# Layer 0's channel-by-row tile: VectorE block transposes of a second load in place of TensorE transposes

## The chip, the cores and the metric

The kernel runs on one core of one Trainium2 chip. The metric is the device time of one execution in microseconds; the time of a kernel is the median of several executions. The core has five engines that run side by side, each through its own queue of instructions in order: TensorE (PE, with its weight loads shown apart as PEld), VectorE (DVE), ScalarE (ACT), GpSimd (POOL) and SyncE (SP), which issues most of the transfers. Transfers of one issuing queue run on 16 shared DMA engines. An instruction waits for semaphores that others set.

## The reference

The input `x` has 128 rows (`s`) of 256 tokens (`i`) of 256 channels. Two layers of the form `x = x + layer(group_norm(x))` follow each other:

```python
# layer 0: 8 heads of 32 channels, bias from z, gate
m_norm = layer_norm(m)                       # m = group_norm(x), 32 groups of 8 channels
q, k, v = m_norm @ Wq.T, m_norm @ Wk.T, m_norm @ Wv.T
b = layer_norm(z) @ Wb.T                     # z: 256 x 256 x 128, one bias per head
p = softmax(q @ k.T / sqrt(32) + b)          # over the 256 tokens of one row s
o = (p @ v) * sigmoid(m @ Wg.T + bg)
x = x + o @ Wo.T + bo
# layer 1: 4 heads of 64 channels, only keys within 16 tokens
x = x + attention(group_norm(x))
```

All numbers are float32. The group norm of layer 0 needs one mean and one scale per channel over the whole of `x`; the layer norm after it needs one root per token (`lrs`).

## The kernel before

The program has a fast path and a general one; a verdict computed at the end of the fast path decides whether the general one runs as well. Only the fast path runs here, and it has four stages.

First, until about 240 us, the stage over `z`: 16 jobs load 2 MB of `z` each, take statistics on DVE (`z_front`), turn the data on PE and project it to the bias (`z_back`), and leave the exponential of the bias in `eb`. Between the jobs `x` is read once for its group moments. Small steps are hung into this stage by a table, `plan`, whose key says after which job and at which quarter of its DVE work a step is issued: among them `norm`, which takes the rows `M0` and `R0` (mean and scale of each channel, the same on all partitions), and the turn of pair 0. Weights are prepared here too.

Second, the loop of layer 0, one iteration for each of the 64 pairs of rows. Its order is written out by hand under a manual schedule: what an engine does follows the order of the calls. Four pairs are under way in an iteration: `old` and `was` are being finished, `now` is in its attention, `nxt` is being prepared, and `nn` is being centred. A pair passes through these steps:

- its construction loads `xt`, 512 rows (tokens) on partitions in four tiles of 128, by one 512 KB DMA (L1225); token 2p+b of a row lies on partition p;
- `centre` and `scale` (L1233, L1236) form `xg` = (x - M) R on POOL;
- `moments` takes mean and variance of each token on DVE, `root` the root on POOL, `send` writes the 512 roots to DRAM (`rs_d`, L1259), and `fetch` reads them back, the same on every partition, as `rs_r` (L1264);
- `turn` makes `xgT`, channels on partitions: eight 128x128 transposes on PE into PSUM tile `ps_x` (L1274), copied out by ACT (L1278);
- `normal` multiplies `xgT` with `rs_r` on POOL (L1283), which gives `xnT`; the weights have been centred, so that subtracting the token's mean isn't needed;
- `project` (L1296) makes `qT` and `kT` from `xnT` and the gate `gT` from `xgT`, `values` (L1311) makes `v` from `xnT`;
- `scores(r, c)` (L1330) and the exponential on ACT (L1337), `add_bias`: product with `eb` on DVE (L1346) and sum over the two token halves on POOL (`eboth`, L1351); `apply` (L1362, L1370) makes the weighted values and the attention sums `su`;
- `gate`, then `invert`: reciprocal of the sums on DVE (L1383), written to DRAM (`rsum`, L1384) and read back by four DMAs as `rvb` (L1391);
- `normalize` on POOL (L1407), `out_row` on PE (L1417), `keep_row` on DVE (L1424), and a 2 MB store of `x1` every fourth pair (L1430).

The scores' PSUM tiles and `ps_x` share two buffers; `xg`, `xgT`, `xnT` and `rs_r` have two buffers each, `xt` five. SP issues in this order in an iteration: roots written, sums written, sums fetched (four), roots fetched, store of `x1` if any, next `xt`.

Third, a short passage with the group moments of layer 1. Fourth, the loop of layer 1. It gets its channel-major tile without PE: `xs` is loaded in runs of 32 channels by four DMAs a pair, one for each band of 32 partitions (L1720), and VectorE's transpose (L1730), which turns 32x32 blocks, finishes it; ACT then subtracts the mean (L1735).

Of the kernel before, what the change touches and what calls it, by code (L numbers as in the profile page):

```python
# [9 lines left out]
F32 = mybir.dt.float32  # L10
AF = mybir.ActivationFunctionType
ALU = mybir.AluOpType
# [4 lines left out]
P = 128  # L17
# [4 lines left out]
def bcast(ap, axis, n):  # L22

    ap = ap.unsqueeze(axis)
    shape = list(ap.shape)
    shape[axis] = n
    return ap.broadcast_to(shape)
# [746 lines left out]
def fast_kernel(  # L774
# [25 lines left out]
    nc = tc.nc  # L800
    S, I, C = x.shape
    CZ = z.shape[2]
    H = wbT.shape[1]
    D0 = C // H
# [3 lines left out]
    NB = I // P  # L808
    KC = C // P
    NP = S // 2  # L810
    N2 = 2 * I
# [4 lines left out]
    const = ctx.enter_context(tc.tile_pool(name="const", bufs=1))  # L816
    dram = ctx.enter_context(tc.tile_pool(name="dram", bufs=1, space=DRAM))

    ident = const.tile([P, P], F32, name="ident")
# [111 lines left out]
    for a in range(KC):  # L931
        for h in range(H1):
            n = P // H1
# [5 lines left out]
    for h in range(H1):  # L939
        n = P // H1  # L940
# [57 lines left out]
    def mm(name):  # L998
        return ps_mm.tile([P, 512], F32, name=name, tag="mm")
# [199 lines left out]
    HQ = P // D0  # L1199
    NT = 2 * NB  # L1200
# [11 lines left out]
    for n in range(RC):  # L1212
# [2 lines left out]
            bcast(ident.rearrange("p (q d) -> p q d", q=HQ)[:, :, n * D0 // RC], 2, D0),  # L1215
        )

    class Pair:


# [7 lines left out]
            )  # L1228


        def centre(self):
            self.xg = la.tile([P, NT, C], F32, name="xg", tag="xg", bufs=2)
            nc.gpsimd.tensor_tensor(self.xg, self.xt, bcast(M0, 1, NT), ALU.subtract)  # L1233

        def scale(self):
# [145 lines left out]
        def invert(self):  # L1381
            rv = self.rv = lb.tile([P, I], F32, name="rv", tag="rv", bufs=2)
            nc.vector.reciprocal(rv, su)  # L1383
            nc.sync.dma_start(  # L1384
                rsum[self.p].rearrange("q r c i -> (q r c) i"), rv[0 : P : D0 // RC]
            )
            if self.p == NP - 1:
                return
            self.rvb = lb.tile([P, 2, KC, I], F32, name="rvb", tag="rvb", bufs=2)
            for q in range(HQ):  # L1390
                nc.sync.dma_start(  # L1391
                    self.rvb[q * D0 : (q + 1) * D0].rearrange("p r c i -> p (r c i)"),
                    rsum[self.p, q].rearrange("r c i -> (r c i)").unsqueeze(0).broadcast_to([D0, RC * I]),
                )
# [67 lines left out]
    def some(n):  # L1462
        for _ in range(min(n, len(later))):
            later.pop(0)()
# [10 lines left out]
    def pair(p):  # L1475
        return Pair(p) if p < NP else Nobody()
# [20 lines left out]
    def norm():  # L1497
        nonlocal M0, R0, nxt
        M0, R0 = next(steps)
        now.centre()  # L1500
        now.scale()
        nxt = pair(1)

    def weigh():
# [5 lines left out]

    plan = {
        (0, 4): begin, (1, 1): lambda: next(steps), (1, 3): lambda: next(steps), (1, 4): take, (2, 3): norm,
        (3, 4): weigh,
        (5, 3): lambda: now.send(nc.scalar),
# [13 lines left out]
    behind, nx, n = None, 0, 0  # L1528
# [39 lines left out]
    su = ps_o.tile([P, I], F32, name="ps_su")  # L1568

    with tc.manual_schedule():  # L1570
        old = was = Nobody()
        es = nn3 = None
        for p in range(NP):

            nxt.root()
            nxt.send()
            e0 = now.add_bias(0, 0, now.scores(0, 0))
            was.apply(1, es)
            was.gate(1)
            was.invert()  # L1580
            nxt.fetch()
            nn.centre()
            if p == 0:
                nxt.residual()
            now.project("qT", 1)
            now.project("kT", 1)
            some(1 if p < NP - 2 else 3)
            now.values(0)
            now.keep_values(0)

            es = e0, now.add_bias(0, 1, now.scores(0, 1))
            nn.scale()
            if p == 0:
                now.residual()
            for m in range(KC):
                now.project("gT", m)
            old.out_row(1)
            some(1 if p < NP - 2 else 3)
            old.keep_row(1)

            nn3 = pair(p + 3)
            e0 = now.add_bias(1, 0, now.scores(1, 0))
            now.apply(0, es)
            now.gate(0)
            nxt.turn()
            nxt.normal()
            was.normalize(0)
            now.values(1)
            now.keep_values(1)
            nn.moments(0)  # L1610
            if p == NP - 1:
                some(8)

            es = e0, now.add_bias(1, 1, now.scores(1, 1))
            was.normalize(1)
            nn.residual()
            nxt.project("qT", 0)
            nxt.project("kT", 0)
            nn.moments(1)
            some(3 if p < NP - 2 else 9)  # L1620
            was.out_row(0)
            was.keep_row(0)
            old, was, now, nxt, nn = was, now, nxt, nn, nn3
        was.apply(1, es)
        was.gate(1)
        was.invert()
        old.out_row(1)
        was.spread()
        old.keep_row(1)
        for r in range(2):  # L1630
            was.normalize_last(r)
        for r in range(2):
            was.out_row(r)
            was.keep_row(r)
        some(len(later))
# [29 lines left out]
    with tc.tile_pool(name="l1", bufs=2) as sb, tc.tile_pool(  # L1665
        name="l1s", bufs=4
    ) as sm, tc.tile_pool(name="ps1_mm", bufs=2, space=PSUM) as ps_mm, tc.tile_pool(
        name="ps1_s", bufs=1, space=PSUM
    ) as ps_s, tc.tile_pool(name="ps1_o", bufs=1, space=PSUM) as ps_o:

        def mm1(name):
            return ps_mm.tile([P, 512], F32, name=name, tag="mm")
# [174 lines left out]
        def pair1(p):  # L1847
            return Pair1(p) if p < NP else Nobody()
# [15 lines left out]
        with tc.manual_schedule():  # L1864
            now, nxt = pair1(0), pair1(1)
# [18 lines left out]
        with tc.manual_schedule():  # L1884
            was = Nobody()
            for p in range(NP - 1):
                nn = pair1(p + 2) if p == 0 else n3
# [27 lines left out]
                was, now, nxt = now, nxt, nn  # L1915
# [19 lines left out]
        ps = mm1("ok_ps")  # L1935
# [4 lines left out]
@with_exitstack  # L1940
def mixer_kernel(ctx, tc, *args):

    nc = tc.nc
    keep = ctx.enter_context(tc.tile_pool(name="verdict", bufs=1))
    verdict = keep.tile([1, 1], mybir.dt.int32, name="verdict")
    fast_kernel(tc, *args, verdict)
    again = nc.values_load(verdict[0:1, 0:1], min_val=0, max_val=1)
    with tc.If(again > 0):
        general_kernel(tc, *args)
# [53 lines left out]
```

## Time and profile before

| what | value |
|---|---|
| time, median of 3 (lowest to highest) | 3313.72 us (3311.55 to 3315.22) |
| the profiled execution's own time | 3316.03 us |
| span of its profile | 3314.3 us |
| mean granted clock of TensorE | 0.982 |
| PE, share of the span | 95% |
| DVE | 64% |
| POOL | 59% |
| ACT | 44% |
| share of PE in the chain that ended last | 91% |

The shares are means over stages that differ. The profile's 40 slices of 83 us each show three parts: two and a half slices in which the DMA engines are nearly full (the stage over `z` and the first reading of `x`), slices 3 to 24 for layer 0, and the rest for layer 1, with a dip of PE between the two layers. The chain of work that ended last is followed back from the last instruction, at each step to what released it, so its lines say what set the time: the projections of layer 0 (L1296) hold 21% of the span in it, the scores (L1330) 8%, and PE's transposes `ps_x` (L1274) 2%.

Of the operations that the change touches, the trace of before has these: 512 transposes on PE, 8 for each of the 64 pairs; 128 copies of `xgT` by ACT, 589 ns each; and, in layer 1, 256 block loads and 64 block transposes.

### The profile page before, as it was taken

The numbers are of one execution on the slowest core, as the hardware profiler recorded it, in microseconds if no ns is written. First come the engines' busy times: TensorE is split into PE (matmuls) and PEld (weight loads), VectorE is DVE, ScalarE is ACT, GpSimd is POOL, SyncE is SP. The second block draws the span as 40 slices with busy tenths as digits, with TensorE's granted clock in tenths as the row PEclk, the third lists the DMA queues.
The fourth block names the chain that finished last, engine by engine and source line by source line (L and its number), as shares of the span: only waits on it lengthen the run. The fifth ranks groups of instructions, "written<-read, shape, count | busy, mean of one in ns | idle before, by whom it ended". The sixth has DMA issues, their size and how long they took to land.

```text
span 3314.3 us, 80768 instructions
## 1 busy us (share of the span) xinstructions
PE 3157.9 (95%) x34656; PEld 1977.2 (60%) x34656; DVE 2121.6 (64%) x3179; ACT 1452.7 (44%) x2121; POOL 1962.8 (59%) x1375
## 2 busy tenths in 40 slices
PE   5389999999999999999999999699999999999998
PEld 3255555555555555555555555466666666666666
DVE  7955666666666666666666666466655555555566
ACT  2264444444444444444444444244444444444443
POOL 2378777777787777787887776233333333333332
PEclk8699999999999999999999999899999999999999
DMA  9951212212221222222122211533333434343431
GB/s 354 375 137 43 75 49 75 75 46 65 72 75 49 75 75 60 64 64 69 49 75 75 75 49 52 104 79 91 85 90 86 92 85 91 85 92 84 92 90 54
DMA packets 464879, 295.92 MB, mean 89 GB/s; under 512 B 312480, under 2 KB 413728, under 8 KB 463360
## 3 DMA queue, kind: packets, MB, share of 16 engines
q1 hardware_dynamic: 459440, 287.76, 31.7%
q8 instruction: 275, 4.51, 0.6%
q10 hardware_dynamic: 5072, 2.90, 0.3%
q14 instruction: 92, 0.75, 0.1%
HBM read 221.85 MB, written 68.75 MB: 88 GB/s over the span
## 4 chain that ended last, share of the span: by engine, by line
PE 91%; DVE 3%; DMA 3%; ACT 1%; POOL 1%; SPq 1%; issue 0%; ACTq 0%; POOLq 0%; DVEq 0%
PE ps_p L1296 21%; PE ps_p L1745 14%; PE ps_sc L1330 8%; PE ps_y L1833 7%; PE ps_ov L1362 7%; PE ps_v L1760 7%; PE ps_y L1417 7%; PE ps_v L1311 6%; PE ps_o L1802 3%; PE ps_su L1370 3%; PE ps_sc L1774 3%; PE ps_x L1274 2%; PE ps_su L1802 1%; DVE st L1178 1%; DVE zst L1103 1%; DMA zt<-in_z_dram 1%
## 5 line engine op out<-in xcount | busy, mean ns | idle before, releaser
L1351 POOL TENSOR_TENSOR eboth<-e 128x512 f32<-128x512 f32 x512 | 640.6, 1273 | 392.9 <-DVE e L1346 389.7
L1346 DVE TENSOR_TENSOR e<-ps_sc,eb 128x1024 f32<-128x1024 f32 x512 | 603.1, 1219 | 307.0 <-ACT ps_sc L1337 306.9
L1337 ACT ACTIVATE ps_sc<-ps_sc 128x1024 f32<-128x1024 f32 x512 | 492.8, 1006 | 509.2 <-PE ps_sc L1330 509.2
L1784 POOL TENSOR_TENSOR e<-e,bw 128x384 f32<-128x384 f32 x256 | 259.5, 1035 | 769.8 <-ACT e L1782 769.8
L1745 PE MATMUL ps_p<-xgT,w_in 128*128 128x512 f32 x1024 | 470.3, 602 | 4.5 <-issue 3.7
L1745 PEld LDWEIGHTS ps_p<-xgT,w_in 128*128 128x128 f32 x1024 | 190.1, 191 | 203.7 <-issue 174.8
L1330 PE MATMUL ps_sc<-qT,kT 32*128 32x256 f32 x4096 | 293.3, 400 | 2.1 <-ACT kT L1300 2.1
L1296 PE MATMUL ps_p<-xnT,wq 128*128 128x512 f32 x512 | 267.3, 634 | 3.5 <-POOL xnT L1283 3.1
L1833 PE MATMUL ps_y<-w_out,oT 128*128 128x256 f32 x1024 | 250.3, 388 | 2.6 <-DVE oT L1818 2.6
L1837 DVE TENSOR_TENSOR yo<-ps_y,xt 128x512 f32<-128x512 f32 x128 | 88.4, 690 | 251.9 <-PE ps_y L1833 149.7
L1362 PE MATMUL ps_ov<-e,v 128*32 128x256 f32 x4096 | 247.7, 382 | 0.0
L1417 PE MATMUL ps_y<-wo,oT 128*128 128x256 f32 x1024 | 242.1, 379 | 2.0 <-POOL oT L1407 1.2
L1417 PEld LDWEIGHTS ps_y<-wo,oT 128*128 128x128 f32 x1024 | 194.3, 190 | 82.5 <-issue 59.3
L1311 PE MATMUL ps_v<-wv,xnT 128*128 128x256 f32 x1024 | 242.2, 379 | 0.0
L1330 PEld LDWEIGHTS ps_sc<-qT,kT 32*128 32x128 f32 x4096 | 184.9, 184 | 94.4 <-issue 83.6
L1296 PE MATMUL ps_p<-xnT,wk 128*128 128x512 f32 x512 | 240.8, 592 | 0.0
L1296 PE MATMUL ps_p<-xgT,wg 128*128 128x512 f32 x512 | 236.8, 605 | 0.0
L1760 PE MATMUL ps_v<-w_in,xgT 128*128 128x256 f32 x1024 | 231.8, 379 | 0.0
L1815 DVE RECIPROCAL rv<-odd 128x256 f32<-128x256 f32 x128 | 224.4, 1753 | 4.4
L1760 PEld LDWEIGHTS ps_v<-w_in,xgT 128*128 128x128 f32 x1024 | 194.4, 190 | 53.5 <-issue 30.1
L1317 DVE TENSOR_TENSOR v<-ps_v,vb_r 128x512 f32<-128x512 f32 x128 | 88.6, 692 | 206.8 <-PE ps_v L1311 206.8
L1311 PEld LDWEIGHTS ps_v<-wv,xnT 128*128 128x128 f32 x1024 | 189.6, 190 | 50.8 <-issue 31.0
(169 smaller groups left out, 4989.9 us busy)
## 6 DMA issues: line engine op xcount, KB each, us to landing
xa<-in_x_dram SPq DMA_DIRECT2D x8, 4096.0 KB
xt<-in_x_dram SPq DMA_DIRECT2D x64, 512.0 KB
x<-xo SPq DMA_DIRECT2D x16, 2048.0 KB
xs<-x SPq DMA_DIRECT2D x256, 128.0 KB
xt<-x SPq DMA_DIRECT2D x64, 512.0 KB
rvb<-rsum SPq DMA_DIRECT2D x252, 128.0 KB
out_dram<-yo SPq DMA_DIRECT2D x63, 512.0 KB
zt<-in_z_dram SPq DMA_DIRECT2D x15, 2048.0 KB
```

The costliest lines, as they stand in the source:

```text
L1296: nc.tensor.matmul(ps, w[:, k, m * P : (m + 1) * P], getattr(self, src)[:, k, :], start=(k == 0), stop=(k == KC - 1),)
L1311: nc.tensor.matmul(self.ps_v[:, b * C : (b + 1) * C], self.xnT[:, k, t * P : (t + 1) * P], wv[:, k, :], start=(k == 0), stop=(k == KC - 1),)
L1330: nc.tensor.matmul(self.pss[q // 2][:, q % 2, b, :], self.kT[rs, c, r * I + b * P : r * I + (b + 1) * P], self.qT[rs, c, r * I : (r + 1) * I],
L1337: nc.scalar.activation(self.pss[a], self.pss[a], AF.Exp)
L1346: nc.vector.tensor_tensor(e, pss[a], eb[:, h : h + 2], ALU.mult)
L1351: nc.gpsimd.tensor_tensor(t, es[a][:, :, 0, :], es[a][:, :, 1, :], ALU.add)
L1362: nc.tensor.matmul(ov[q * D0 : (q + 1) * D0, c, :], self.v[:, r, b, h * D0 : (h + 1) * D0], es[q // 2][:, q % 2, b, :], start=(b == 0), st ...
L1417: nc.tensor.matmul(self.ps_y[:, b * C : (b + 1) * C], self.oT[r][:, k, b * P : (b + 1) * P], wo[:, k, :], start=(k == 0), stop=(k == KC - 1),)
L1745: nc.tensor.matmul(ps, w_in[:, k, n * C + m * P : n * C + (m + 1) * P], self.xgT[:, k, :], start=(k == 0), stop=(k == KC - 1),)
L1760: nc.tensor.matmul(ps[:, b * C : (b + 1) * C], self.xgT[:, k, t * P : (t + 1) * P], w_in[:, k, 2 * C : 3 * C], start=(k == 0), stop=(k == ...
L1784: nc.gpsimd.tensor_tensor(e[:, q], e[:, q], bcast(bw.rearrange("p b w -> p (b w)"), 1, KC), ALU.mult)
L1833: nc.tensor.matmul(ps[:, b * C : (b + 1) * C], self.oT[r][:, k, b * P : (b + 1) * P], w_out[:, k, :], start=(k == 0), stop=(k == KC - 1),)
```

## The change

Layer 0 gets its channel-major tile in the way that layer 1 does. Each pair from the second on is loaded a second time, as `xs`, in runs of 32 channels (`blocks`: four DMAs of 128 KB); two VectorE transposes make `xgT` from it (`turn_blocks`), and ACT applies the group norm, R x - R M, with its per-partition scale and bias (`scale_blocks`). For that, R and -R M are needed as columns: `norm` makes them in `col` by four products on PE and two small DVE instructions. `turn` is no longer called in the loop; pair 0 is still turned on PE in the stage over `z`. `xg` remains, for the statistics of the tokens, with one buffer instead of two. `xs` has one buffer: the block load of `nn` is issued after the transposes of `nxt`. The loop's order changes in three more places: `normal` comes before `scores(1, 0)` instead of after `gate(0)`; `invert` ends with the write of the sums, and their four fetches form `fetch_sums`, called after `fetch`.

```diff
+    col = const.tile([P, 2, KC], F32, name="col")
...
+        def blocks(self):
+            self.xs = la.tile([P, NB, KC, 2 * HQ, D0], F32, name="xs", tag="xs", bufs=1)
+            by_block = x[2 * self.p : 2 * self.p + 2].rearrange(
+                "s (i b n) (k j a) -> j b (n k) (s i) a", i=HQ, n=NB, k=KC, a=D0
+            )
+            for j in range(HQ):
+                nc.sync.dma_start(self.xs[j * D0 : (j + 1) * D0].rearrange("b n k i a -> b (n k) i a"), by_block[j])
+
+        def turn_blocks(self):
+            self.xgT = la.tile([P, KC, N2], F32, name="xgT", tag="xgT", bufs=2)
+            for n in range(NB):
+                nc.vector.transpose(
+                    self.xgT.rearrange("p k (s n i b) -> p n k s i b", s=2, n=NB, i=HQ)[:, n],
+                    self.xs[:, n].rearrange("p k (s i) a -> p k s i a", s=2),
+                )
+
+        def scale_blocks(self):
+            for k in range(KC):
+                nc.scalar.activation(
+                    self.xgT[:, k, :], self.xgT[:, k, :], AF.Identity,
+                    bias=col[:, 1, k : k + 1], scale=col[:, 0, k : k + 1],
+                )
...
-            self.xg = la.tile([P, NT, C], F32, name="xg", tag="xg", bufs=2)
+            self.xg = la.tile([P, NT, C], F32, name="xg", tag="xg", bufs=1)
...
-            if self.p == NP - 1:
-                return
+
+        def fetch_sums(self):
             self.rvb = lb.tile([P, 2, KC, I], F32, name="rvb", tag="rvb", bufs=2)
...
         M0, R0 = next(steps)
+        ps = mm("ps_col")
+        for n, row in enumerate((R0, M0)):
+            for k in range(KC):
+                nc.tensor.matmul(
+                    ps[:, n * KC + k : n * KC + k + 1], row[:, k * P : (k + 1) * P], ident[:, 0:1],
+                    start=True, stop=True,
+                )
+        nc.vector.tensor_copy(col[:, 0], ps[:, 0:KC])
+        nc.vector.scalar_tensor_tensor(col[:, 1], ps[:, KC : 2 * KC], -1.0, col[:, 0], ALU.mult, ALU.mult)
...
     with tc.manual_schedule():
+        nxt.blocks()
...
             nxt.fetch()
+            was.fetch_sums()
             nn.centre()
...
             now.keep_values(0)
+            nxt.turn_blocks()
+            nn.blocks()
...
                 now.project("gT", m)
+            nxt.scale_blocks()
...
+            nxt.normal()
             e0 = now.add_bias(1, 0, now.scores(1, 0))
             now.apply(0, es)
             now.gate(0)
-            nxt.turn()
-            nxt.normal()
             was.normalize(0)
```

## The prediction

> **What bounds the kernel now.** I read the windows view first, for the stretch in which layer 0 runs its loop over pairs of rows. Its columns are busy time and instruction counts of PE, PEld, DVE, ACT and POOL, then the granted clock, the DMA share and GB/s.
>
> ```profile
> 330.00:2038.00 1708.00, 1707.15 (x13259) 1000.24 (x13258) 1136.27 (x1718) 764.99 (x950) 1350.32 (x947) 1.00 0.23 65
> ```
>
> PE has work in 1707.15 of 1708.00 us at full clock; POOL has 79%, DVE 67%, ACT 45%, the DMA engines 23%. A busy PE is not always an advancing PE, so I next read the timeline of one pair (start, duration, engine, line, operation), and took from it the distances between the starts of PE's groups.
>
> ```profile
> 1004.30 1.05 PE L1370 MATMUL ps_su<-eboth,pick 128*32 128x256 f32 x16
> 1005.28 1.09 PE L1274 MATMUL ps_x<-ident,xg 128*128 128x128 f32 x8
> 1006.21 1.89 PE L1311 MATMUL ps_v<-wv,xnT 128*128 128x256 f32 x8
> 1008.03 1.15 PE L1330 MATMUL ps_sc<-qT,kT 32*128 32x256 f32 x16
> 1009.11 2.17 PE L1296 MATMUL ps_p<-xnT,wq 128*128 128x512 f32 x4
> 1010.16 0.30 PEld L1296 LDWEIGHTS ps_p<-xnT,wq 128*128 128x128 f32 x2 [0.75 <-POOL xnT L1283]
> 1011.12 1.88 PE L1296 MATMUL ps_p<-xnT,wk 128*128 128x512 f32 x4
> ...
> 1018.46 1.98 PE L1296 MATMUL ps_p<-xnT,wq 128*128 128x512 f32 x4
> 1020.28 1.88 PE L1296 MATMUL ps_p<-xnT,wk 128*128 128x512 f32 x4
> ```
>
> Two things are to be seen. The eight transposes hold PE from 1005.28 to 1006.21, 0.93 us. The wait ahead of them is nothing: from the sums' start to theirs is 0.98 us, and where `wq` follows the sums (1017.48 to 1018.46, same view) it is also 0.98. And the first `wq` group takes 2.01 us (1009.11 to 1011.12) where the other takes 1.82: it waits 0.19 us for the second half of `xnT`. The same groups return every 28.77 us, all through the loop, so PE's order of work sets this stage, and only what shortens that order counts.
>
> **What the Trainium skill says.** "VectorE: DVE Perf Modes", section "The three transpose paths": VectorE turns 32x32 blocks only, into SBUF. That is why the load must place 32-channel runs on four bands of partitions; layer 1 of this trace does the same (L1720, L1730). Same page, section on the TRN2 errata: an instruction with SBUF sources pays a fixed latency, so that half a tile costs more than half; its formula for another operation, (N+151)/0.96, gives as an estimate 0.69 us for 512 elements. No row here shows a 512-element block transpose. "DMA: Bandwidth & Descriptors", section "Why small descriptors are slow": a fixed overhead per packet. Layer 1's 128-byte packets show its size here: in one pair (2600 to 2618.6 us) 4096 of them took 55.0 us together, 13.4 ns each. Same page, section "Anatomy of one DMA — SWDGE (gpsimd) path": completion of a write to HBM waits for its receipt. The trace agrees: `rs_d`, issued at 1018.68, is complete at 1026.86 by its semaphore, 8.2 us for 2 KB.
>
> **The change, part by part.** The slots it uses in the same pair:
>
> ```profile
> 1023.93 0.69 DVE L1317 TENSOR_TENSOR v<-ps_v,vb_r 128x512 f32<-128x512 f32 x1 [2.15 <-PE ps_v L1311]
> ...
> 1026.11 2.36 DVE L1346 TENSOR_TENSOR e<-ps_sc,eb 128x1024 f32<-128x1024 f32 x2 [1.49 <-ACT ps_sc L1337]
> ...
> 1028.63 0.69 ACT L1300 ACTIVATE gT<-ps_p,bg_c 128x512 f32<-128x512 f32 x1 [1.03 <-PE ps_p L1296]
> 1029.68 0.37 SPq L1264 DMA_DIRECT2D rs_r<-rs_d  x1
> 1029.93 2.36 POOL L1236 TENSOR_TENSOR xg<-xg,R_l 128x1024 f32<-128x1024 f32 x1
> 1030.25 1.15 PE L1330 MATMUL ps_sc<-qT,kT 32*128 32x256 f32 x16
> ```
>
> *TensorE transposes out.* 63 loop iterations turn a next pair (pair 0 keeps its turn): 63 x 0.93 = 58.6 us less.
>
> *`normal` moved up,* past `scores(1,0)` and the bias product, on POOL past the two `eboth` sums of (1,0). It now starts when `scale` ends, 1032.3, and ends at 1034.8; PE wants `xnT` at about 1036.9. The 0.19 us wait goes: 62 x 0.2 = 12.4 us. The first pair has a larger one: `xnT` there ends at 263.0 and PE starts `wq` at 261.86 instead of about 259.1; with `normal` 2.5 us earlier, 2.7 us come back. The `eboth` pair is 2.5 us later; PE reads it in the next iteration's `apply(1)`, some 8 us on. `normalize(0)` behind it ends at about 1038.6, with `out_row(0)` due at 1040.0: 1.4 us cover; without it, PE waits one for one.
>
> *DVE block transposes.* The whole-tile one of layer 1 takes 1.235 us:
>
> ```profile
> L1730 DVE STREAM_TRANSPOSE xT<-xs x64: 1229/1235/1245, 2104.8 to 3251.7; 128x1024 f32<-128x1024 f32 x64
> L1720 SPq DMA_DIRECT2D xs<-x x256: 562/829/4164, 2098.4 to 3238.0; - x128
> ```
>
> Two halves cost 1.24 us (exactly half each) to 2.47 (no saving); I take 2 x 0.70 = 1.4. DVE stands idle 1.49 us in that slot, waiting for ACT. What is queued behind is the bias product of (0,1), ended at 1028.47; `scores(1,0)` needs its PSUM at 1030.25, so there are 1.78 us more. Cost nothing up to 3.27 us, that is at both ends.
>
> *ACT.* Two copies of 589 ns go, two scalings come. The nearest row is L1735, 717 ns, which reads SBUF and adds a bias; bounds 0.59 to 1.0 us, I take 0.717. They run from 1029.32 to 1030.8; the next exponentials become ready at 1031.4. Hidden; at 1.0 us also.
>
> *The block load.* Four DMAs a pair, 0.829 us of SP each, 3.3 us. SP stands idle from about 1031.5 to the next root at 1047.5. Behind them on SP stand the store of x1 (one pair in four) and the load of `xt`, first read by the next iteration's `centre`, at about 1049. Transfer: 55.0/16 = 3.4 us of all engines; 23% of 28.77 = 6.6 us becomes 10. `xs` has one buffer: reload starts at about 1029.7 and must land before the next turn, 22 us on. Bounds: 13.4 ns a packet to 86 (below, rival D).
>
> *`fetch` before the sums' fetches.* `rs_d` is complete at 1026.86, `rsum` at 1027.85. So `rs_r` is issued at 1026.9 instead of 1029.68, and the four `rvb` fetches stay where `rsum` puts them. `rs_r` lands at about 1030; `normal` wants it at 1032.3. Without that move it would have landed at 1033.4 and stalled POOL by 1.1 us.
>
> *`xg` with one buffer.* `centre` waits for the last statistics of the pair before; the root ahead of it on POOL already does. Nothing.
>
> *Ahead of the loop.* `norm` puts four one-column products on PE before a group of z transposes that started at 175.34. Their rows R and M are written by DVE at 178.0, and the like at L1692 took 1.93 us for its eight records. So PE, on the chain there, is up to 4.6 us late, DVE idle meanwhile. The chain then runs into a z load (203.23, 16.76 us) whose queue was full. Bounds 0 to 5 us; I take 2.
>
> Sum: -58.6 - 12.4 - 2.7 + 2 = -71.7. The profiled execution took 3316.03 us (span 3314.3, 1.7 around it), so 3244.3. The median shown, 3313.72, is 2.3 lower: 3242.
>
> **Rivals.** *B, the small wait stays:* `xnT`, or `normalize(0)` behind it, still holds PE about 0.2 us a pair. For: covers of 1.4 to 2.1 us on POOL, 79% busy. Against: POOL does no more work than before. 62 x 0.2 = 12.4 less gain: 3254. *C, a slot overflows:* DVE or ACT pushes the exponential chain, or fetches land late in some pairs, half a microsecond a pair: 63 x 0.5 = 31 less gain, 3273. For: the DVE slot has 0.1 us to spare at my price. Against: 1.78 us behind it. *D, slower:* the queue. The block loads stand in one queue with the tiny `rs_d` write, on the path root, write (8.2 us), fetch, `normal`, `wq`. I count 3.7 us of margin on that path (2.3 before `normal` is late, 1.4 more before `normalize(0)` holds PE), and 1.1 us of gain per pair: beyond 4.8 us of added delay the kernel is slower, 63 us per further microsecond; at 7 us, 3314 + 2.2 x 63 = 3452. In packets: 27.65 - 6.6 = 21 us of DMA time free, so 82 ns a packet fills the period and 86 undoes the gain. For: the 8.2 us of that write. Against: 13.4 ns in layer 1, and the write comes 13 us after the loads were issued. *E, the change doesn't do what it says:* eight of 512 transposes stay; excluded by the code.
>
> **How the numbers follow.** The main case 0.70 (own range 3235 to 3250), B 0.14, C 0.09, D 0.07. Faster by over 0.2% (about what a measurement can tell from no change, 6.6 us) holds in all of A, B, C: 0.93; D is split 0.05 slower, 0.02 within. Below, the gain can't much exceed 76 us (no cost ahead of the loop, and small waits elsewhere): with some room, 3234. Above, B whole and part of C: 3268.
>
> **What would show it.** Right: the period of PE's groups 27.65 us; no L1274 in the loop; `wq` 1.82 us both times; two STREAM_TRANSPOSE of about 0.7 us in DVE's slot and no longer gap before `ps_sc`; DMA share about 0.36. Wrong: PEld waiting for POOL `xnT` or `oT`; POOL waiting for a DMA `rs_r`; DVE waiting for a DMA `xs`; a start of the loop later than 240.3 by more than 5 us.

## The result, and the profile after

The changed kernel takes 3253.89 us (median of four, 3252.30 to 3256.59). The kernel before takes 3312.64 us (median of four, 3310.42 to 3315.22). The ratio is 0.9823, with a 95% interval of 0.9806 to 0.9840: about 59 us, or 1.8%, less. The forecast was 3242, with a range of 3234 to 3268.

The profiled execution took 3252.30 us (span 3250.6), against 3316.03 (span 3314.3) for the one of before. This is the head of its page.

```profile
span 3250.6 us, 80098 instructions
PE 3093.1 (95%) x34160; PEld 1930.1 (59%) x34160; DVE 2201.7 (68%) x3307; ACT 1473.0 (45%) x2121; POOL 1961.6 (60%) x1375
```

The windows view over layer 0's loop (busy time and count of PE, PEld, DVE, ACT, POOL, then clock, DMA share, GB/s) has PE still without a gap, and the DMA share at 0.38 instead of 0.23; 0.36 was forecast.

```profile
330.00:1980.00 1650.00, 1649.90 (x12818) 958.06 (x12820) 1212.93 (x1839) 786.64 (x953) 1351.12 (x948) 1.00 0.38 87
```

The timeline of one pair (start, duration, engine, line, operation, idle time before and its releaser), cut to PE's groups and to what the change moved:

```profile
1001.24 1.29 DVE L1245 STREAM_TRANSPOSE xgT<-xs 128x512 f32<-128x512 f32 x2
1002.82 2.36 DVE L1372 TENSOR_TENSOR e<-ps_sc,eb 128x1024 f32<-128x1024 f32 x2 [0.28 <-ACT ps_sc L1363]
1004.63 0.34 SPq L1290 DMA_DIRECT2D rs_r<-rs_d  x1
1005.06 1.77 SPq L1417 DMA_DIRECT2D rvb<-rsum  x4
1005.92 1.51 ACT L1252 ACTIVATE xgT<-xgT,col 128x512 f32<-128x512 f32 x2
1006.93 6.18 SPq L1240 DMA_DIRECT2D xs<-in_x_dram  x4
1009.79 1.05 PE L1396 MATMUL ps_su<-eboth,pick 128*32 128x256 f32 x16
1010.76 2.00 PE L1337 MATMUL ps_v<-wv,xnT 128*128 128x256 f32 x8
1012.69 1.15 PE L1356 MATMUL ps_sc<-qT,kT 32*128 32x256 f32 x16
1013.76 1.98 PE L1322 MATMUL ps_p<-xnT,wq 128*128 128x512 f32 x4
1015.58 1.88 PE L1322 MATMUL ps_p<-xnT,wk 128*128 128x512 f32 x4
...
1022.92 1.98 PE L1322 MATMUL ps_p<-xnT,wq 128*128 128x512 f32 x4
```

Three things are to be seen. The values product `ps_v` now follows the sums directly, and no transposes stand between. The first `wq` group takes 1.82 us (1013.76 to 1015.58), as forecast. And the transposes sit in DVE's old gap, which shrinks from 1.49 us to 0.28. The groups return every 27.75 us, where they did every 28.77.

What DVE and ACT do instead shows in the answers for the two lines (duration in ns: lowest, median, highest):

```profile
L1245 DVE STREAM_TRANSPOSE xgT<-xs x126: 667/684/703, 253.2 to 1973.3; 128x512 f32<-128x512 f32 x126
L1252 ACT ACTIVATE xgT<-xgT,col x126: 801/802/806, 257.9 to 1978.1; 128x512 f32<-128x512 f32 x126
```

I took the time between the two profiled executions apart, 3316.03 - 3252.30 = 63.7 us. From the first scores to the last output row, the loop of layer 0 went from 1846.5 to 1779.8 us: 66.7 less. It starts at 246.0 instead of 240.3: 5.7 more. What follows it takes 2.7 us less (1224.7 instead of 1227.5, each rounded). That is scatter and no effect of the change that could be told: `fetch_only` below, which has the code of before from there on, takes 1224.7 us as well, and `best_again`, which has the changed code there, 1227.2. Inside the loop, the distances between the starts of PE's groups add up like this:

| group | change over the loop, us |
|---|---|
| transposes `ps_x`, gone | -58.5 |
| `wq` | -13.5 |
| scores (most of it in the first pair) | -2.2 |
| `ps_v` | +6.4 |
| `wk` and the rest | +1.1 |
| sum | -66.7 |

`ps_v` was not in my sum at all. There was also a wait that I had listed as a sign of being wrong. This is the view of waits from 300 to 1990 us (waiting engine, tile and line, releaser: us in total, times, longest):

```profile
POOL xnT L1309 <- DMA rs_r<-rs_d: 45.7, 46, 2.3
...
POOL xnT L1309 <- ACT ps_sc L1363: 12.6, 12, 1.2
...
PEld ps_y L1443 <- POOL oT L1433: 3.4, 8, 0.9
```

POOL waits for the fetched roots in 46 pairs, about 1 us each time. The view puts twelve further waits of `normal` down to ACT. By the landing times (from the trace's semaphore updates) the roots end these too: `normal` starts within 0.2 us of the landing of its roots in 60 of the 63 pairs. PE hardly waits for POOL behind it. I had expected the fetch to land 2.3 us ahead of its use.

### The profile page after: what moved, and what is told of

Same layout as the page of the kernel before. It is cut to its first block, busy times and chain, and to the rows that moved or that the text cites. A ratio compares the mean times of both kernels' runs of the same rounds, so it can differ in the third digit from the quotient of the medians.

```text
span 3250.6 us, 80098 instructions
## 1 busy us (share of the span) xinstructions
PE 3093.1 (95%) x34160; PEld 1930.1 (59%) x34160; DVE 2201.7 (68%) x3307; ACT 1473.0 (45%) x2121; POOL 1961.6 (60%) x1375
## 4 chain that ended last, share of the span: by engine, by line
PE 91%; DVE 4%; DMA 3%; ACT 1%; SPq 1%; issue 0%; POOL 0%; ACTq 0%; DVEq 0%; POOLq 0%
PE ps_p L1322 21%; PE ps_p L1784 14%; PE ps_sc L1356 8%; PE ps_y L1872 7%; PE ps_ov L1388 7%; PE ps_v L1337 7%; PE ps_v L1799 7%; PE ps_y L1443 7%; PE ps_o L1841 4%; PE ps_su L1396 3%; PE ps_sc L1813 3%; PE ps_su L1841 1%; DVE st L1178 1%; DMA zt<-in_z_dram 1%; DVE zst L1103 1%; DMA xa<-in_x_dram 1%
## 5 line engine op out<-in xcount | busy, mean ns | idle before, releaser
L1322 PE MATMUL ps_p<-xnT,wq 128*128 128x512 f32 x512 | 255.7, 622 | 1.2 <-POOL xnT L1309 1.1
L1443 PE MATMUL ps_y<-wo,oT 128*128 128x256 f32 x1024 | 242.4, 380 | 2.8 <-POOL oT L1433 2.0
L1872 PEld LDWEIGHTS ps_y<-w_out,oT 128*128 128x128 f32 x1024 | 189.3, 190 | 35.6 <-issue 3.4
```

The costliest lines, as they stand in the source:

```text
L1322: nc.tensor.matmul(ps, w[:, k, m * P : (m + 1) * P], getattr(self, src)[:, k, :], start=(k == 0), stop=(k == KC - 1),)
L1443: nc.tensor.matmul(self.ps_y[:, b * C : (b + 1) * C], self.oT[r][:, k, b * P : (b + 1) * P], wo[:, k, :], start=(k == 0), stop=(k == KC - 1),)
L1872: nc.tensor.matmul(ps[:, b * C : (b + 1) * C], self.oT[r][:, k, b * P : (b + 1) * P], w_out[:, k, :], start=(k == 0), stop=(k == KC - 1),)
```

## The experiments

**Do the columns cost time ahead of the loop?** `norm` asks PE for four products, two for each of the rows R and M, as soon as it is called; the trace records each of them twice. In the timeline of the changed kernel PE stands 2.63 us for the rows and then needs about 0.9 us for the products, ahead of a group of z transposes:

```profile
178.81 0.28 DVE L990 COPY R_l<-rs_l 128x256 f32<-128x256 f32 x1
...
179.15 0.61 PE L1529 MATMUL ps_col<-ident,R_l 128*128 128x1 f32 x4 [2.63 <-DVE R_l L990]
...
180.06 2.02 PE L1125 MATMUL ps_t<-ident,zt 128*128 128x128 f32 x16
```

The edit issues the same products at a later step of the plan, (3, 1), and DVE's two instructions at the head of `weigh`, (3, 4):

```diff
         M0, R0 = next(steps)
-        ps = mm("ps_col")
...
-        nc.vector.tensor_copy(col[:, 0], ps[:, 0:KC])
-        nc.vector.scalar_tensor_tensor(col[:, 1], ps[:, KC : 2 * KC], -1.0, col[:, 0], ALU.mult, ALU.mult)
         now.centre()
...
+    def columns():
+        nonlocal ps_col
+        ps = ps_col = mm("ps_col")
...
+        nc.vector.tensor_copy(col[:, 0], ps_col[:, 0:KC])
+        nc.vector.scalar_tensor_tensor(col[:, 1], ps_col[:, KC : 2 * KC], -1.0, col[:, 0], ALU.mult, ALU.mult)
...
-        (3, 4): weigh,
+        (3, 1): columns, (3, 4): weigh,
```

> The changed kernel with the four one-column products issued one job of the z stage later, when their rows have long been written; the two small VectorE instructions follow three quarters of a job after them. Theory (in the changed kernel PE stands 2.6 us waiting for the rows and about 1 us in the products, and the whole stage is late by that): PE passes the place with about 1 us, the first scores of the loop start near 242 us instead of 246.0, and the time falls by 3 to 5 us, to about 3250. Rival (the loop starts late because the first block load's four transfers stand between the z loads): the start stays near 246 and the time near 3254.

Measured: 3248.93 us (3248.0 to 3252.12, five), ratio 0.9806 (0.9792 to 0.9819). The loop starts at 243.1, its period is 27.75. In its timeline the products come without a wait for DVE:

```profile
184.26 0.61 PE L1535 MATMUL ps_col<-ident,R_l 128*128 128x1 f32 x4
184.73 0.58 PE L1535 MATMUL ps_col<-ident,M_l 128*128 128x1 f32 x4
```

So the wait was on the path. How it reaches the loop shows in SP's waits over the whole changed kernel: the loads of `z` wait for PE's z transposes.

```profile
SPq L1090 <- PE ps_t L1125: 46.1, 7, 13.0
```

| us | z transposes start ahead of the place, behind it | next `z` load issued | last `z` load landed | first scores |
|---|---|---|---|---|
| before | 172.4, 175.3 | 181.7 | 220.0 | 240.3 |
| after | 173.5, 180.1 | 186.4 | 224.2 | 246.0 |
| columns late | 174.1, 177.0 | 183.4 | 222.9 | 243.1 |

A single start scatters: in the seven executions here that keep the changed kernel's code up to the loop it lies between 244.3 and 248.0 us (mean 246.1), in the three with this edit between 241.7 and 243.1 (mean 242.4), in the two with the code of before at 240.3 and 239.6. The columns' early place thus costs some 3.7 us of the 6.1 by which the start moved in the mean. At their late place the products still take their own time: the two groups of z transposes around them start 5.2 us apart instead of 4.3. One of pair 1's four block loads, which are issued already in the stage over `z`, also changed its place among the z loads (from 186.8 to 206.2 us), so the edit is not quite isolated. But with the edit the `z` load of the table left 3.0 us earlier, before either of these places; so the expectation's rival did not bring these 3.0 us, though a smaller part of it further on is not excluded. Of the 2.4 us that remain in the mean, the products' own 0.9 are a part; the rest stays open.

**Is the gain the transposes' alone?** The edit puts `normal` back behind `gate(0)`; PE's transposes stay out.

```diff
-            nxt.normal()
             e0 = now.add_bias(1, 0, now.scores(1, 0))
             now.apply(0, es)
             now.gate(0)
+            nxt.normal()
```

> The changed kernel with normal put back behind apply and gate of the first row, everything else as changed. My forecast priced the move of normal at the 0.19 us wait alone: then 62 x 0.2 = 12 us more, about 3266, a period of 27.95 us. Rival: without the transposes PE reaches the q projection 0.83 us earlier, while xnT ends when it did before, so nearly the whole gain of the transposes turns into a wait: a period of 28.7 us, PEld waiting for POOL xnT about 0.9 us a pair, about 3313.

Measured: 3321.2 us (one run), period 28.75; its loop starts at 247.5. The rival is right. The timeline shows why:

```profile
1013.77 2.49 POOL L1377 TENSOR_TENSOR eboth<-e 128x512 f32<-128x512 f32 x2 [1.62 <-DVE e L1372]
...
1016.23 2.49 POOL L1309 TENSOR_TENSOR xnT<-xgT,rs_r 128x512 f32<-128x512 f32 x2
...
1017.54 2.35 PE L1322 MATMUL ps_p<-xnT,wq 128*128 128x512 f32 x4 [0.56 <-POOL xnT L1309]
```

`normal` stands behind both `eboth` sums and starts at 1016.23; PE has no transposes left to do, so it comes to `wq` sooner and waits 0.56 us, then again for the second half. Its view of waits:

```profile
PEld ps_p L1322 <- POOL xnT L1309: 111.2, 117, 1.3
```

The scores-to-`wq` distance is 1.70 us instead of 1.08, and `wq` itself 0.37 longer: 1.0 us a pair, all that the transposes give. I had priced the move at 0.2 us a pair, which was the wait of before. With PE one step shorter, the move decides whether there is a gain.

**What is 0.93 us of transposes worth?** My theory, formed from the trace after, was that the first full-width group behind the narrow ones (the sums' products are 32 columns wide, the scores' 32 rows deep) pays 0.10 us, whoever it is: `ps_x` before, `ps_v` now. The edit puts eight transposes of `nn`'s `xg` back behind `gate(0)`, into a PSUM tile that nobody reads, and leaves all else.

```diff
+        def turn_idle(self):
+            ps = ps_s.tile([P, KC, N2], F32, name="ps_x", tag="s")
+            for k in range(KC):
+                for t in range(NT):
+                    nc.tensor.transpose(
+                        ps[:, k, t * P : (t + 1) * P], self.xg[:, t, k * P : (k + 1) * P], ident
+                    )
...
             now.gate(0)
+            nn.turn_idle()
```

> The changed kernel with the eight PE transposes left in the loop at their old place (62 pairs), into a PSUM tile that nobody reads; they are work added, the result isn't used. Theory (the first full-width group after the narrow sums costs 0.10 us more, whichever group it is, and the transposes had been carrying that): transposes 0.93 us from start to start, values(1) back from 1.93 to 1.82, period 28.58 us, 62 x 0.83 = 51 us more, about 3305. Rival (as in my sum, the whole 0.93 is the transposes'; the 0.1 in values(1) comes from elsewhere): values(1) stays at 1.93, period 28.68, 58 us more, about 3312.

Measured: 3303.97 us (one run), period 28.58, where 27.75 + 0.93 - 0.10 = 28.58. `ps_v` is back at 1.82 us (5.56 to 7.38):

```profile
1003.65 1.05 PE L1404 MATMUL ps_su<-eboth,pick 128*32 128x256 f32 x16
1004.63 1.09 PE L1310 MATMUL ps_x<-ident,xg 128*128 128x128 f32 x8
1005.56 1.89 PE L1345 MATMUL ps_v<-wv,xnT 128*128 128x256 f32 x8
1007.38 1.15 PE L1364 MATMUL ps_sc<-qT,kT 32*128 32x256 f32 x16
```

So eight transposes between the sums and the values are worth 0.83 us, not the 0.93 that they occupy. The two gate products `wg` show the same in the traces of before and after: they are alike but for their neighbour, and the one behind the scores takes 1.82 us, the one behind the other 1.72. "TensorEngine Tiling (Array Packing)", section "Tiling Modes", says that a change of the tiling mode drains TensorE. The trace agrees that such a change costs something, about 0.10 us here, and shows it on the group that follows; whether a drain is the reason no run tells.

**What is the fetch's new place worth?** The edit sends the sums' fetches ahead of the roots' fetch again.

```diff
             was.invert()
-            nxt.fetch()
             was.fetch_sums()
+            nxt.fetch()
```

> The changed kernel with the fetch of the rows' roots put back behind the four fetches of the sums. Theory (the landing moves with the issue, 2.3 us): normal starts up to 2.3 us later, normalize(0) behind it has 0.5 us of cover in the trace of the changed kernel, PE then waits up to 1.8 us a pair at the out row: up to 110 us more, about 3360. Rival (the roots' and the sums' fetches share one stretch of the queue, so that the landing moves by little; or POOL's idle time takes it): within 0.5 us a pair, no more than 3285, and unchanged at best.

Measured: 3330.25 us (3328.7 to 3331.25, four), ratio 1.0051 (1.0035 to 1.0066): slower than the kernel before, beyond the rival's 3285 and within what the theory allowed, though by another path than either, as will be seen. The mean period is 28.94, and it changes from pair to pair between 27.75 and 30.6. Its view of waits:

```profile
POOL xnT L1309 <- DMA rs_r<-rs_d: 180.2, 58, 4.8
...
PEld ps_y L1443 <- POOL oT L1433: 76.1, 58, 1.7
...
PEld ps_p L1322 <- POOL xnT L1309: 54.1, 75, 1.7
```

The landing times, taken from the trace's semaphore updates and counted from the issue of the roots' write (`rs_d`), show how little had moved (medians over all 63 fetches):

| us | `rs_d` complete | `rs_r` issued | `rs_r` landed | `rvb` landed |
|---|---|---|---|---|
| before | 8.38 | 11.12 | 15.18 | 13.96 |
| after | 8.40 | 8.42 | 14.06 | 16.47 |
| fetch put back | 8.49 | 11.25 | 15.47 | 14.07 |

Issued 2.7 us earlier, the roots land 1.1 us earlier. The fetch then takes 5.5 us instead of 3.9, and the sums' fetches land 2.5 us later. Yet 1.4 us of landing time (14.06 to 15.47) makes 76 us over the kernel. The 3.7 us of margin that I had counted along one iteration can't give that, so I looked for a loop. In the changed kernel's pair at 1010 us, POOL works from `normal` to the next root without a gap (the first line puts the wait down to ACT, but ACT's scaling had ended at 1007.43, and the roots landed at 1010.03, 0.13 us ahead of `normal`):

```profile
1010.16 2.51 POOL L1309 TENSOR_TENSOR xnT<-xgT,rs_r 128x512 f32<-128x512 f32 x2 [1.16 <-ACT ps_sc L1363]
1012.62 2.50 POOL L1377 TENSOR_TENSOR eboth<-e 128x512 f32<-128x512 f32 x2
1015.07 1.28 POOL L1433 TENSOR_TENSOR oT<-oT,rvb 128x512 f32<-128x512 f32 x1
1016.30 2.50 POOL L1377 TENSOR_TENSOR eboth<-e 128x512 f32<-128x512 f32 x2
1018.75 1.28 POOL L1433 TENSOR_TENSOR oT<-oT,rvb 128x512 f32<-128x512 f32 x1
1019.97 2.38 POOL L1265 TENSOR_TENSOR xt<-xt,bo_r 128x1024 f32<-128x1024 f32 x1
1022.32 1.01 POOL L1282 TENSOR_TENSOR lrs<-lrs,mhalf 128x4 f32<-128x4 f32 x1
1023.36 0.38 SPq L1285 DMA_DIRECT2D rs_d<-lrs  x1
```

From `normal` to the root it is 1022.32 - 1010.16 = 12.16 us; from the root to its write 1.04; from the write's issue to the landed fetch 14.06 (the median of the table); from there to the next `normal` 0.13. Together 27.4 us a turn, against the 27.75 that PE needs: 0.36 us of slack, once round the loop. In the kernel before, `normal` stood behind the `eboth` pair, so its part of the loop was 10.0 us, and the turn was 10.0 + 1.04 + 15.18 + 0.13 = 26.4 against 28.77. With the fetch put back it is 12.16 + 1.04 + 15.47 + 0.13 = 28.8, more than PE's 27.75.

The trace of that run shows the loop closed. `normal` starts within 0.2 us of the landing in 61 of 63 pairs, and from `normal` to the next write of roots it is 13.17 to 13.24 us in every pair but the first: by as much as a landing is late, so is the next write. The means are 15.60 us to the landing, 0.14 to `normal` and 13.21 to the next write; before rounding they add up to 28.94, the mean period. In the changed kernel the last part varies from 13.20 to 14.32: there is the slack.

**Is it this loop?** If so, taking any work off it must give the gain back. The edit keeps the fetch in its late place, and moves `residual` (2.38 us on POOL between `normal` and the root) out of the loop, to where POOL has centred `nn`.

```diff
             was.invert()
+            was.fetch_sums()
             nxt.fetch()
-            was.fetch_sums()
             nn.centre()
-            if p == 0:
-                nxt.residual()
+            nxt.residual()
...
-            nn.residual()
```

> The kernel of the run before (the changed one with the roots' fetch behind the sums' fetches, 3330 us), with one more edit: residual, 2.38 us of POOL, no longer ahead of the next root but after the next iteration's centre. Theory (a loop through POOL and the transfers sets the pace there: root, send, 15.3 us to the landing of the roots, normal, eboth, normalize, eboth, normalize, residual, next root, together about 28.8 us against PE's 27.75): without the residual the loop is about 26.4 us, PE is the bound again, period 27.75, time 3250 to 3258. Rival (the roots' late landing as such holds PE, wherever the next root stands): period stays near 28.9, about 3330.

Measured: 3251.2 us (3250.38 to 3253.69, four), ratio 0.9813 (0.9798 to 0.9828), period 27.75, though the roots land as late as they did (15.7 us after their write's issue). Two edits that do nothing together, and one of which costs 76 us alone: that is the loop, 28.8 - 2.4 = 26.4 us.

```profile
POOL xnT L1309 <- DMA rs_r<-rs_d: 17.0, 20, 3.1
```

**Is an earlier fetch worth anything without the rest?** The kernel before, with only the order of the two fetches changed (for that, `invert` is split as in the change):

```diff
-            if self.p == NP - 1:
-                return
+
+        def fetch_sums(self):
...
             nxt.fetch()
+            was.fetch_sums()
```

> The kernel before with one part of the change alone: the roots' fetch ahead of the sums' four fetches. Theory (the loop through POOL and the transfers is about 26 us there, PE's period 28.77, and normal is late in the iteration): no change, 3311 to 3316. Rival (the 0.19 us wait for xnT comes from the roots): it goes, 62 x 0.19 = 12 us, 3301.

Measured: 3310.67 us (3309.19 to 3313.82, twelve), ratio 0.9992 (0.9983 to 1.0000): no change that can be told. It is as the sum of that loop says, 26.4 us before this edit, with room to PE's 28.77.

**How much room has DVE's slot?** The two block transposes are done three times over, with the same result.

```diff
-            for n in range(NB):
+            for n in (0, 1) * 3:
```

> The changed kernel with the two VectorE block transposes done three times, the same result written again: 2.6 us more on VectorE in the slot ahead of the bias product of (0,1). My forecast counted no cost up to 3.27 us in that slot; three times 1.29 is 3.87. Theory A (only the PSUM of the scores (1,0) counts, as in the forecast): 0.5 to 0.6 us a pair, 3285 to 3292. Theory B (the bias product's lateness goes on through eboth and scale to normal and then round the POOL loop): 1 us or more a pair, over 3310. No cost (3254) would mean that the slot is wider than the trace shows.

Measured: 3271.8 us (one run), period 27.99. Its timeline:

```profile
1009.94 3.67 DVE L1245 STREAM_TRANSPOSE xgT<-xs 128x512 f32<-128x512 f32 x6
...
1013.53 2.32 DVE L1372 TENSOR_TENSOR e<-ps_sc,eb 128x1024 f32<-128x1024 f32 x2
...
1015.66 1.38 PE L1356 MATMUL ps_sc<-qT,kT 32*128 32x256 f32 x16
```

Six in a row take 3.67 us, 0.61 each, and 3.67 - 3.27 = 0.40 us run over the room that I had counted (3.27). The kernel is 17.9 us slower than the changed one, less than either theory said. In this slot the scores take 1.31 us instead of 1.08, and these 0.23 us are nearly the whole by which the period grew. The mechanism is as forecast and the room within 0.2 us of it; the duration that I scaled from one pair of transposes was too large.

**Is the queue harmless?** The block load in runs of 32 bytes, by four times the transfers and packets.

```diff
-                nc.sync.dma_start(self.xs[j * D0 : (j + 1) * D0].rearrange("b n k i a -> b (n k) i a"), by_block[j])
+                for a in range(0, D0, 8):
+                    nc.sync.dma_start(
+                        self.xs[j * D0 : (j + 1) * D0].rearrange("b n k i a -> b (n k) i a")[:, :, :, a : a + 8],
+                        by_block[j][:, :, :, a : a + 8],
+                    )
```

> The changed kernel with every block load cut into 16 transfers of 32-byte runs instead of four of 128-byte runs: 16384 packets a pair, the same bytes. Theory (rival D of the forecast is far from its threshold: the block loads come after the fetches and are done before the next send): period 27.75 to 27.9, at most 3262. Rival D (the block loads delay the small writes and fetches behind them, or SP is still issuing them when the next root is ready): rs_d or rs_r land later, every further microsecond costs 63 us; over 3290.

Measured: 3386.42 us (one run). The period is 29.9 in the mean and uneven, up to 36.6. SP's timeline:

```profile
1034.25 14.67 SPq L1241 DMA_DIRECT2D xs<-in_x_dram  x16
1049.02 1.59 SPq L1227 DMA_DIRECT2D xt<-in_x_dram  x1
1050.71 0.42 SPq L1289 DMA_DIRECT2D rs_d<-lrs  x1
```

Its waits:

```profile
POOL xg L1263 <- DMA xt<-in_x_dram: 191.9, 46, 12.4
...
POOL xnT L1313 <- DMA rs_r<-rs_d: 111.3, 45, 5.1
```

SP is busy for 14.67 us with sixteen transfers, and what stands behind them, the load of the next `xt` and the roots' write, leaves late. `xt` costs POOL more than the roots do. The theory is refuted for this size; the mechanism of rival D exists, one step on. Packets and transfers were multiplied together, so which of the two costs how much stays open. Here `rs_d` itself is complete 10.0 us after its issue. At the changed kernel's 128-byte runs that is not there: 8.40 us, against 8.38 before.

**A version that gains from both.** The columns late and `residual` off the loop, the fetch at its new place:

```diff
-        (3, 4): weigh,
+        (3, 1): columns, (3, 4): weigh,
...
-            if p == 0:
-                nxt.residual()
+            nxt.residual()
...
-            nn.residual()
```

> The version with the column products one job later (3248.9 us), with residual moved behind the next iteration's centre as well. Theory (PE sets the period already, the POOL loop is about 0.25 us below it): the waits of POOL for the roots go, the period stays 27.75, and only the few pairs with a longer period come down to it: 3246 to 3249. Rival (POOL's loop still costs something in every pair): period under 27.75, more than 5 us faster.

Measured: 3248.2 us (3246.73 to 3249.95, five), ratio 0.9802 (0.9788 to 0.9815). POOL's wait for the roots is gone, but the period stays 27.75, as it must if PE sets it:

```profile
POOL xnT L1309 <- DMA rs_r<-rs_d: 0.6, 1, 0.6
```

To set it against the changed kernel itself, I ran both once more, side by side on one chip.

> The changed kernel once more, beside the next run on the same chip: 3252 to 3256, ratio to the kernel before 0.982 to 0.983.

> The changed kernel with the column products one job later and the residual behind the next iteration's centre, once more beside the changed kernel: 4 to 7 us faster than it, 3247 to 3249, from the earlier start of the loop alone; the period stays 27.75.

Measured: the changed kernel again 3251.57 us (3250.83 to 3255.46, five; ratio 0.9821, 0.9807 to 0.9834), the version 3248.69 (3247.74 to 3249.97, five; ratio 0.9807, 0.9794 to 0.9821). It is 2.9 us (0.09%) faster in the medians, the two ranges don't overlap, and this is less than I expected. The intervals of the two ratios overlap. Its loop starts at 242.4 where the changed kernel's started at 244.4 beside it, and takes 1778.3 us against 1779.9.

## Why the prediction was right, and where it was not

The forecast was 11.9 us low: inside the stated range, but above the 3235 to 3250 that I gave the main case. It was the allowance for rivals B and C that held it, and neither of their mechanisms came, so that the range held is in part luck. I made the forecast against a profiled execution: 3244.3 forecast, 3252.3 measured, 8.0 us. The other 3.9 is a matter of medians: the execution of before lay 2.3 us above the median that it stood with, that of after lies 1.6 below its own. The 8.0 are 6.4 (`ps_v`), 3.7 (start of the loop), -2.7 (after the loop, scatter) and 0.6 of small rests.

- *"TensorE transposes out", 63 x 0.93: the step that failed.* The 0.93 us did go (-58.5). But the group behind it became dearer, 1.82 to 1.93 (+6.4 over the loop), so the term was 0.83 a pair. The profile of before had the number: `wq` behind narrow groups takes 1.82 us, and `wk` behind `wq` takes 1.72; and so for the two `wg`. I used the 0.98 from the sums to the next group to show that no wait lay ahead of the transposes, and did not ask what the next full-width group pays when they are gone. The period came to 27.75 instead of 27.65 for this alone.
- *"`normal` moved up", 62 x 0.2.* Right in size: `wq` -13.5, and the first pair's period 3.77 us shorter (27.73 to 23.96), where 0.93 and 2.7 were forecast. Wrong in meaning: priced as the wait of before, it is in fact the condition of the whole gain (3321.2 us without it).
- *DVE, 2 x 0.70.* 0.684 each, and no wait of PE from it. The estimate from "VectorE: DVE Perf Modes" (section on the TRN2 errata), 0.69 for 512 elements, agrees. The room, 3.27 us, holds within 0.2 us, as the thrice-done transposes show.
- *ACT, 0.717.* It is 0.802. The row that I took adds a bias only, this one has a scale as well and works in place; which of the two it is that costs stays open. Inside the bounds, and hidden.
- *The block load.* DMA share 0.38 for 0.36; `rs_d` and `rsum` complete as before. (13.4 ns is the whole time of a packet; what part of it is a fixed overhead no run here shows.) Rival D did not come at this size.
- *"`rs_r` lands at about 1030".* Wrong. I moved the landing by as much as the issue, 2.8 us; in the trace it moved by 1.1. The 2.3 us of cover ahead of `normal` were not there, and POOL's wait, which I listed as a sign of being wrong, appeared in nearly every pair. It cost PE next to nothing, with 0.36 us to spare a turn: that the gain stood was luck as far as this path goes, for I had not counted it.
- *Rival D's margin, 3.7 us (4.8 until slower).* Wrong in kind. I followed the roots once through an iteration. The path closes on itself through POOL: moving `normal` ahead of the `eboth` pair put 2.2 us more work between `normal` and the next root. A delay of 1.4 us, well under 3.7, already makes the kernel slower than before. So the chance that I gave to trouble from this side, 0.07, rested on a margin that is about a tenth as wide as I wrote.
- *Ahead of the loop, 2 of 0 to 5.* 5.7 measured, beyond my bound. A later start than 240.3 by more than 5 us was another of my signs of being wrong, and it appeared. The 2.63 us wait is on the path, and no full queue absorbs it, because the loads of `z` wait for PE; of the 4.6 us that I had as the most, I let only 2 through. Of the 5.7, 4.2 are there when the last `z` load lands (224.2 against 220.0). In the other twelve executions the first scores follow that landing by 19.5 to 20.3 us, with either code; in this one by 21.8, and there the granted clock was lower for longer. These are the windows of before (first two) and after:

```profile
225.00:235.00 10.00, 4.75 (x21) 1.38 (x22) 1.44 (x7) 5.04 (x13) 9.26 (x4) 0.66 0.01 2
235.00:240.00 5.00, 4.02 (x12) 1.76 (x12) 2.49 (x12) 3.36 (x10) 3.28 (x2) 1.00 0.00 0
```

```profile
229.00:239.00 10.00, 4.69 (x20) 1.32 (x20) 1.66 (x8) 4.93 (x13) 9.04 (x4) 0.70 0.01 2
239.00:246.00 7.00, 6.09 (x12) 2.83 (x12) 2.73 (x13) 3.81 (x11) 4.51 (x3) 0.70 0.00 0
```

That is 0.34 x 10 = 3.4 us of clock withheld before and 0.30 x 17 = 5.1 after. The other executions with the changed code up to the loop have 1.7 or 3.4, so this part belongs to one execution and not to the change. No experiment sets that clock, so the link is argued.

The measured time is the very number of rival B (3254), but not by its mechanism, nor is C's (3273) there: PE does not wait 0.2 us a pair for POOL (PEld's wait for `oT` is 3.4 us in all), and no slot overflows.

## What to carry to other kernels

When a group is taken out of a full engine, price it as the difference between two orders of work: what the next group costs behind the new neighbour counts too, and so does which wait now decides the moment at which it may start. A software-pipelined loop that sends data through DRAM should be summed once round, through every engine and transfer, and compared with the period of the engine that sets it: cover within one iteration did not show it here. And an earlier issue of a transfer need not be an equally earlier landing: here 2.7 us of the one made 1.1 of the other, with four fetches issued right behind it; why, no run separates.

## What the runs showed of the hardware that was not expected

- The first full-width PE group after groups 32 rows or 32 columns wide takes about 0.10 us longer (`ps_v` 1.93 against 1.82 us; `wg` 1.82 behind the scores against 1.72 behind `wg`).
- The roots' fetch (`rs_r`), issued 2.7 us earlier, with the sums' four fetches issued right behind it instead of ahead of it, took 5.5 us instead of 3.9 to land.
- A VectorE block transpose of 128x512 float32 takes 0.684 us; two in a row take 1.29 together, six 3.67. The one of 128x1024 took 1.235.
- SP was busy for 14.67 us with sixteen transfers of 32-byte runs, and for 6.18 with four of 128-byte runs, in the pairs shown; the median of one is 0.674 us in both kernels.
